# Cross attention on one Trainium2 core: the context turned by VectorE in 32x32 blocks, scores in four row groups, scores emitted ahead of the previous pair's weighted sum

## The chip, the cores and the metric

The kernel runs on one core of one Trainium2 chip. The metric is the device time of one execution in microseconds (us), and lower is better. TensorE (PE in the profile) multiplies matrices; PEld is its weight load. VectorE is DVE, ScalarE is ACT, GpSimd is POOL, and SP is the engine whose queue issues most of the transfers here. All of the data are float32 apart from the mask. A difference of less than about 0.3% can't be told from no change.

## The reference, cut to what matters

There are 32 sequences of 56 tokens with width 256, and each has its own context of 1500 rows by 256. Two layers run one after the other.

- Layer 0 first computes a decayed running sum over the context, projects its mean over time, adds it to every token of the sequence and normalises. Then comes a mixture of 16 experts of width 176, of which each token uses its six best.
- Layer 1 first attends from the tokens to the context, as below, and then uses the better of two experts of width 1024.

```python
scores = jnp.einsum('bsd,bmd->bsm', hidden_states, memory_tokens) * scale
scores = jnp.where(memory_mask[:, None, :], scores, neg_inf)
attn = jax.nn.softmax(scores, axis=-1)
readout = jnp.einsum('bsm,bmd->bsd', attn, memory_tokens)
```

The scores sum over the width (256), the readout sums over the context rows (1500). TensorE sums over the partitions of its operands, so the scores want the context with the width on the partitions, and the readout wants it with the rows on the partitions.

## The kernel before, in words

**Tiling.** Two sequences make a pair: rows 0 to 55 and 64 to 119 of a tile of 128 partitions. There are 16 pairs, in four groups of four. The residual of all tokens stays in SBUF (`xr`).

**Stage 1, the loads and the decayed sum (L123 to L281).** All 32 contexts are loaded once (`load_ctx`, L91), each with two transfers: 128 partitions with 11 rows of the context each, and 92 partitions with one row each. Four buffers take turns. For each context 12 matmuls in four column groups of the array add to `acc` (L205). The weights of layer 0's experts load in between (L200). A chain of small steps then gives the summary that L273 to L281 add to the tokens and normalise.

**Stage 2, layer 0's experts (L291, L384 to L449).** For each group of four pairs, 22 tiles of hidden units go through two matmul groups (L302), a SiLU on ScalarE (L307), two products on VectorE (L308, L310) and the projection back (L315). A float32 matmul shows as two instructions in the profile. The experts' weights per token are spread over the partitions by transfers on SP's queue, six tiles ahead (`cwb`). At a group's end the tokens are normalised, turned by TensorE and copied into `xnp` (L446), the queries of the attention, with the width on the partitions.

**Stage 3, the attention (L460 to L576).** For each pair:

- `transposed` (L469) turns each of the two contexts: 24 TensorE transposes of 128x128 each (L477) into PSUM, and six copies into `cT` by ScalarE (L486) and VectorE (L484).
- `mask_terms` (L489) loads the mask with two transfers, and POOL makes 0 or -1e30 of it (`mf`).
- `scores` (L505): three column blocks of at most 512, in two halves of the width, for the two sequences in the two column halves of the array (L514). VectorE adds the mask and takes the maximum (L520).
- `attend` (L527): the exponential on ScalarE (L530), 12 TensorE transposes of the weights (L541), VectorE's copies into `pT` (L545, L550), 24 matmuls with the context (L555), and the scaled sum into `xr` (L561). Then the next contexts but one are loaded into the freed buffers.

The Tile scheduler orders the instructions of each engine by its own simulation of the program. In the order that it gives to TensorE here, the transposes of the next pair's contexts stand among the steps of the current pair.

**Stage 4, layer 1's experts** (L580 to L620), with the same functions as stage 2, and the output.

**What sets the order around the change.** SP's queue issues the loads of contexts, masks and `cwb` in one order, and a transfer that has to wait for its buffer holds up those behind it. VectorE, ScalarE and POOL also take their instructions strictly in order.

## Time and profile before

| what | value |
|---|---|
| device time, median of three runs | 1325.13 us (1322.62 to 1326.71) |
| profiled execution: span | 1323.2 us |
| its own time | not given beside the span; the median of the runs lies 1.9 us above the span |
| PE busy | 1160.0 us, 88% of the span |
| DVE, ACT, POOL busy | 452.5, 250.5, 70.4 us |
| first context transpose of stage 3 (L477) | 658.78 us |
| last step of stage 3 (L561) | 1008.97 to 1009.45 us |
| contexts moved | 143.79 MB in all, of which 32 x 1.5 MB in stage 1 and again in stage 3 |

The span is the profiled execution from its first to its last instruction. A group's mean is the time of one instruction; on PE these overlap, so that busy time divided by count is less than the mean. PEclk is the share of its full clock that TensorE was granted.

### The profile page before, as it was taken

How to read it: one execution, taken by the hardware profiler on the slowest of the kernel's cores; microseconds unless marked ns; L12 is line 12 of the kernel's file. 1: busy time of each engine (PE TensorE's matmuls, PEld its weight loads, DVE VectorE, ACT ScalarE, POOL GpSimd, SP SyncE). 2: the span in 40 equal slices, each digit the busy share in tenths (PEclk: the TensorE clock that was granted, in tenths of full speed). 3: DMA queues.
4: the chain of work that ended last, by engine and by line, in shares of the span. 5: the costliest groups of instructions: out<-in, count | busy, mean ns of one | idle time of the engine just before them, and what ended most of it. 6: DMA issues, size and time to landing. Idle time of an engine off the chain costs nothing. (4 is left out here: it accounts for less than half of the span.)

```text
span 1323.2 us, 13044 instructions
## 1 busy us (share of the span) xinstructions
PE 1160.0 (88%) x5104; PEld 623.1 (47%) x5104; DVE 452.5 (34%) x1166; ACT 250.5 (19%) x412; POOL 70.4 (5%) x81
## 2 busy tenths in 40 slices
PE   5534455899999999999999998989898999999998
PEld 3111122455555555555445555656564545555554
DVE  2400008622532442332343443433434323232322
ACT  0000000211311321121143332323322111121111
POOL 1300002100000000000021011010100000000000
PEclk9576775799999999999999999999999999999999
DMA  9999990111111111111055345352520001000000
GB/s 304 332 340 338 346 321 35 49 65 56 42 50 51 47 50 49 49 53 53 18 204 198 145 154 185 113 189 108 192 94 15 15 0 28 0 28 1 14 0 14
DMA packets 38445, 143.79 MB, mean 109 GB/s; under 512 B 5031, under 2 KB 29168, under 8 KB 29424
## 3 DMA queue, kind: packets, MB, share of 16 engines
q1 hardware_dynamic: 35122, 134.03, 28.9%
q0 software_dynamic: 432, 6.29, 1.2%
q10 hardware_dynamic: 2830, 2.64, 0.8%
q8 instruction: 40, 0.66, 0.2%
q14 instruction: 21, 0.17, 0.0%
HBM read 140.98 MB, written 1.96 MB: 108 GB/s over the span
## 5 line engine op out<-in xcount | busy, mean ns | idle before, releaser
L302 PE MATMUL gp<-xnT,wg_sb 128*128 128x448 f32 x608 | 258.0, 543 | 0.0
L302 PE MATMUL up<-xnT,wu_sb 128*128 128x448 f32 x608 | 254.9, 540 | 0.0
L315 PE MATMUL y<-hh,wd_sb 128*128 128x448 f32 x608 | 254.3, 541 | 0.0
L308 DVE TENSOR_TENSOR sg<-sg,up 128x448 f32<-128x448 f32 x152 | 94.2, 620 | 422.0 <-PE up L302 417.3
L307 ACT ACTIVATE sg<-gp 128x448 f32<-128x448 f32 x152 | 82.3, 543 | 525.5 <-PE gp L302 517.8
L315 PEld LDWEIGHTS y<-hh,wd_sb 128*128 128x128 f32 x608 | 114.0, 190 | 112.4 <-issue 105.4
L302 PEld LDWEIGHTS up<-xnT,wu_sb 128*128 128x128 f32 x608 | 114.4, 191 | 106.7 <-issue 106.7
L205 PE MATMUL acc<-ctx,cz 128*32 128x256 f32 (+1 forms) x768 | 82.3, 562 | 93.7 <-DMA ctx<-in_cx 93.4
L302 PEld LDWEIGHTS gp<-xnT,wg_sb 128*128 128x128 f32 x608 | 113.7, 191 | 101.8 <-issue 101.8
L477 PE MATMUL tp<-ident,ctx 128*128 128x128 f32 (+1 forms) x768 | 113.5, 284 | 19.9 <-DMA ctx<-in_cx 10.8
L477 PEld LDWEIGHTS tp<-ident,ctx 128*128 128x128 f32 (+1 forms) x768 | 86.0, 145 | 63.1 <-ACT cT L486 18.4
L514 PE MATMUL sp<-cT,xnp 128*64 128x512 f32 (+1 forms) x384 | 103.0, 586 | 0.8 <-DVE mx L520 0.8
L205 PEld LDWEIGHTS acc<-ctx,cz 128*32 128x32 f32 (+1 forms) x768 | 32.5, 148 | 142.2 <-DMA ctx<-in_cx 119.3
L555 PE MATMUL op<-ctx,pT 128*64 128x256 f32 (+1 forms) x768 | 99.2, 387 | 0.0
L310 DVE TENSOR_TENSOR hh<-sg,cwb 128x448 f32<-128x448 f32 x152 | 94.8, 624 | 5.7 <-DMA cwb<-cw 1.0
L486 ACT COPY cT<-tp 128x512 f32<-128x512 f32 (+1 forms) x128 | 71.7, 569 | 96.0 <-PE tp L477 93.0
L555 PEld LDWEIGHTS op<-ctx,pT 128*64 128x64 f32 (+1 forms) x768 | 55.6, 138 | 31.1 <-issue 5.7
L484 DVE COPY cT<-tp 128x512 f32<-128x512 f32 x64 | 44.1, 689 | 73.1 <-PE tp L477 73.1
L514 PEld LDWEIGHTS sp<-cT,xnp 128*64 128x64 f32 x384 | 34.1, 136 | 47.1 <-issue 43.0
L110 ACT ACTIVATE rs<-mv,eps 128x4 f32<-128x4 f32 x20 | 5.9, 297 | 242.8 <-DVE mv L109 242.7
L530 ACT ACTIVATE sc<-sc,nb 128x1500 f32<-128x1500 f32 x16 | 24.8, 1547 | 118.6 <-DVE nb L529 118.6
L497 POOL TENSOR_SCALAR mf<-mu 128x1408 f32<-128x1408 uint8 x16 | 32.7, 2045 | 257.5 <-DVE mx L520 240.4
(116 smaller groups left out, 545.4 us busy)
## 6 DMA issues: line engine op xcount, KB each, us to landing
ctx<-in_cx SPq DMA_DIRECT2D x64, 1408.0 KB
cwb<-cw SPq DMA_DIRECT2D x40, 224.0 KB
ctx<-in_cx SPq DMA_DIRECT2D x64, 92.0 KB
cwb<-cw SPq DMA_DIRECT2D x16, 196.0 KB
mu<-in_mask SPq DMA_DIRECT2D x32, 93.8 KB
wg_sb<-in_wg SPq DMA_DIRECT2D x1, 2816.0 KB
wu_sb<-in_wu SPq DMA_DIRECT2D x1, 2816.0 KB
wd_sb<-in_wd SPq DMA_DIRECT2D x1, 2816.0 KB
```

The source lines that it names most:

```text
L205: PE.matmul(acc[32 * g : 32 * g + 32, :], lhsT=cz[0:r, j, B - 1 - b : 2 * B - 1 - b], rhs=c[0:r, j, :], start=(b == 0 and m == 0), stop=(b ...
L302: PE.matmul(o, lhsT=w[:, k, i * P : (i + 1) * P], rhs=xnT[:, k, :], start=(k == 0), stop=(k == KD - 1),)
L307: A.activation(sg, gp, AF.Silu)
L308: V.tensor_tensor(sg, sg, up, ALU.mult)
L310: V.tensor_tensor(hh, sg, weight(i), ALU.mult)
L315: PE.matmul(ys[k], lhsT=wd[:, i - 1, k * P : (k + 1) * P], rhs=hh, start=(i == 1), stop=(i == nf),)
L477: PE.transpose(tp[:, jj * P : jj * P + r], c[0:r, 4 * n + jj, k * P : (k + 1) * P], ident[0:r, 0:r],)
L484: V.tensor_copy(dst, tp[:, 0 : widths[n]])
L486: A.copy(dst, tp[:, 0 : widths[n]])
L497: G.tensor_scalar(mf[:, 0:TM].rearrange("q (j p) -> q j p", p=P), mu[:, 0:TM].rearrange("q (p j) -> q j p", j=TA), -1.0, BIG, ALU.add, ALU ...
L514: PE.matmul(sp[64 * h : 64 * h + 64, 0:w], lhsT=xnp[:, k, p * P + 64 * h : p * P + 64 * h + 64], rhs=cTs[h][:, k, cols], start=(k == 0), s ...
L555: PE.matmul(op[64 * h : 64 * h + 64, :], lhsT=pT[0:r, j, 64 * h : 64 * h + 64], rhs=ctxs[2 * p + h][0:r, j, :], start=(j == 0), stop=(j == ...
```

## The change

It is in stages 1 and 3, with a new transfer at the end of each group of stage 2.

- The context rows are laid out differently: row t = 12 p + j lies on partition p of 125, chunk j of 12. A load is now 112 partitions and 13 partitions of 12288 bytes each. Six fixed buffers replace four, and POOL sets their partitions 96 to 127 to zero once at the start.
- `transposed` becomes one VectorE instruction for each sequence and half of the width, four for a pair: each block of 32 partitions by 32 columns is turned in place. Afterwards partition 32 a + i holds column i of a 32-wide slice of the width, for the context rows of partition group a. So TensorE's transposes of the context, and ScalarE's and VectorE's copies of them, go.
- The scores now sum over 32 partitions at a time: eight slices e of the width, two sequences h, four row groups a, 64 matmuls of 384 (or 348) columns for a pair, into four PSUM tiles, one for each row group. The masked maximum is four VectorE instructions for a pair instead of three.
- The queries must stand on all four row groups in slices of 32. They go through DRAM: 16 writes at the ends of stage 2's groups (`xd`), and four reads for each pair (`queries`).
- The copies into `pT` move from VectorE to ScalarE, and `mf` has one buffer instead of two.
- TensorE's order in stage 3 is written out by hand: scores of pair p, weighted sum of pair p - 1, transposes of pair p's weights. The other engines' order is still the scheduler's.
- In stage 1 the summary is spread with two matmuls for each pair against a column of the identity, and the selection matrix that VectorE built before (`selb`) goes.

```diff
-    cpool = ctx.enter_context(tc.tile_pool(name="ctx", bufs=4))
+    cpool = ctx.enter_context(tc.tile_pool(name="ctx", bufs=1))
...
+    xd = dram.tile([D, NP, P], F32, name="xd")
+
+    cbuf = [cpool.tile([P, NCH, D], F32, tag=f"ctx{i}", name=f"ctx{i}") for i in range(NCTX)]
+    for c in cbuf:
+        G.memset(c[3 * Q : P], 0.0)
...
     def load_ctx(b):
-        c = cpool.tile([P, NCH, D], F32, tag="ctx", name=f"ctx{b}")
-        nc.sync.dma_start(
-            out=c[:, 0:TA, :], in_=cx[b, 0:TM, :].rearrange("(p j) d -> p j d", j=TA)
-        )
-        nc.sync.dma_start(out=c[0:TR, TA, :], in_=cx[b, TM:T, :])
+        c = cbuf[loads[0] % NCTX]
+        loads[0] += 1
+        cb = cx[b].rearrange("(p j) d -> p j d", j=NCH)
+        nc.sync.dma_start(out=c[0:TS], in_=cb[0:TS])
+        nc.sync.dma_start(out=c[TS:TP], in_=cb[TS:TP])
         return c
...
-                    A.copy(
-                        xnp[:, :, p * P : (p + 1) * P],
-                        tp[:, 0:D].rearrange("p (k c) -> p k c", c=P),
+                    xt = wk.tile([P, KD, P], F32, tag="xt", name="xt")
+                    A.copy(xt, tp[:, 0:D].rearrange("p (k c) -> p k c", c=P))
+                    nc.sync.dma_start(
+                        out=xd[:, GP * g + q, :].rearrange("(k p) c -> p k c", p=P), in_=xt
                     )
...
+        def transposed(b, n):
+            cT = ctp.tile([P, NCH, NE // 2, Q], F32, tag="cT", name="cT")
+            V.transpose(
+                out=cT.rearrange("p j e q -> p j (e q)"),
+                in_=ctxs[b][:, :, P * n : P * n + P],
+            )
             return cT
 
+        def queries(p):
+            xq = at2.tile([P, NE, P], F32, tag="xq", name="xq")
+            for a in range(4):
+                nc.sync.dma_start(
+                    out=xq[Q * a : Q * a + Q, :, :],
+                    in_=xd[:, p, :].rearrange("(e q) c -> q e c", q=Q),
+                )
+            return xq
...
+        def scores(p, cTs, xq, mf):
+            sps = [psc.tile([P, 512], F32, tag=f"sp{a}", name=f"sp{a}") for a in range(4)]
+            for e in range(NE):
+                for h in range(2):
+                    for a in range(4):
                         PE.matmul(
+                            sps[a][64 * h : 64 * h + 64, 0 : NCH * QT[a]],
+                            lhsT=xq[Q * a : Q * a + Q, e, 64 * h : 64 * h + 64],
+                            rhs=cTs[e // 4][h][Q * a : Q * a + Q, :, e % 4, 0 : QT[a]],
+                            start=(e == 0), stop=(e == NE - 1),
                         )
...
+        def turned(sc):
             pT = at.tile([P, NCH, P], F32, tag="pT", name="pT")
             for n in range(3):
                 tp = ppt.tile([P, 512], F32, tag="pt", name="tp")
                 for jj in range(4):
+                    PE.transpose(tp[0:TP, jj * P : (jj + 1) * P], sc[:, 4 * n + jj, :], ident)
+                A.copy(
+                    pT[0:TP, 4 * n : 4 * n + 4, :].rearrange("p j c -> p (j c)"), tp[0:TP, :]
+                )
+            return pT
...
+        with tc.manual_schedule(engines={mybir.EngineType.PE}):
+            before = None
+            for p in range(NP):
+                xq, mf = queries(p), mask_terms(p)
+                cTs = [[transposed(2 * p + h, n) for h in range(2)] for n in range(2)]
+                sc, mx = scores(p, cTs, xq, mf)
+                nb = softmax(sc, mx)
+                if before:
+                    attend(*before)
+                before = (p, turned(sc), nb)
+            attend(*before)
```

Here NCH = 12, TP = 125, Q = 32, NE = 8, TS = 112, NCTX = 6 and QT = [32, 32, 32, 29]. The tile pool of `cT` has four buffers, which is one pair's worth, that of the score tiles one for each row group.

## The prediction, made before the changed kernel ran

> **What bounds it now.** I read the busy times by stage first (columns: window, its length, busy time and count of each engine, granted TensorE clock, DMA share, GB/s).

> ```profile
> 0.00:196.00 196.00, 90.98 (x805) 40.95 (x806) 25.12 (x85) 3.96 (x7) 17.16 (x28) 0.71 0.93 329
> 238.00:658.00 420.00, 419.11 (x1215) 216.96 (x1214) 148.43 (x376) 81.71 (x135) 0.00 (x0) 0.99 0.16 49
> 658.00:1009.00 351.00, 323.03 (x2130) 195.57 (x2128) 141.86 (x378) 110.45 (x178) 39.74 (x36) 0.98 0.41 150
> 1009.00:1323.00 314.00, 306.86 (x912) 158.52 (x912) 102.01 (x225) 52.88 (x87) 0.00 (x0) 1.00 0.04 12
> ```

> Stage 1 waits for loads (DMA 0.93), stages 2 and 4 for TensorE. So does the attention (351 us, PE 92% busy, DVE 40%), and only there is something large removed. Next, that stage's groups of instructions by shape (busy us, mean ns | idle before):

> ```profile
> L477 PE MATMUL tp<-ident,ctx 128*128 128x128 f32 x704 | 109.1, 287 | 19.9 <-DMA ctx<-in_cx 10.8 <-DVE cT L484 6.5 <-ACT cT L486 1.8
> L555 PE MATMUL op<-ctx,pT 128*64 128x256 f32 x704 | 92.1, 388 | 0.0
> L514 PE MATMUL sp<-cT,xnp 128*64 128x512 f32 x256 | 74.4, 597 | 0.8 <-DVE mx L520 0.8
> L530 ACT ACTIVATE sc<-sc,nb 128x1500 f32<-128x1500 f32 x16 | 24.8, 1547 | 118.6 <-DVE nb L529 118.6
> L545 DVE COPY pT<-tp 128x512 f32<-128x512 f32 x32 | 21.3, 686 | 5.5 <-PE tp L541 5.3
> L545 DVE COPY pT<-tp 128x384 f32<-128x384 f32 x16 | 8.8, 552 | 3.1 <-PE tp L541 2.9
> ```

> Then one pair in order of time (start, duration):

> ```profile
> 782.23 1.07 PE L477 MATMUL tp<-ident,ctx 128*128 128x128 f32 x8 [0.80 <-DMA ctx<-in_cx]
> ...
> 792.63 5.18 PE L555 MATMUL op<-ctx,pT 128*64 128x256 f32 x45
> ...
> 797.66 0.34 SPq L93 DMA_DIRECT2D ctx<-in_cx  x1
> 797.86 5.20 PE L514 MATMUL sp<-cT,xnp 128*64 128x512 f32 x21
> ...
> 803.90 1.07 PE L477 MATMUL tp<-ident,ctx 128*128 128x128 f32 x8 [0.85 <-DMA ctx<-in_cx]
> 804.28 1.55 ACT L530 ACTIVATE sc<-sc,nb 128x1500 f32<-128x1500 f32 x1 [10.99 <-DVE nb L529]
> 805.97 0.77 PE L541 MATMUL tp<-ident,sc 128*128 128x128 f32 x5 [1.00 <-ACT sc L530]
> ```

> A pair takes 803.90 - 782.23 = 21.7 us (351 / 16 = 21.9 with the start and the end). TensorE's own prices: at 640 us four full-array matmuls of 448 columns start every 1.51 us, 0.84 ns a column, so a 128-column transpose costs 0.107 us; with two column groups side by side (L514, L555) a 512-column instruction costs 0.215, a 256-column one 0.108. Per pair: scores 24 x 0.215 = 5.2, context transposes 48 x 0.107 = 5.1, weight transposes 12 x 0.107 = 1.3, weighted sum 48 x 0.108 = 5.2, together 16.8; the rest is waits between steps. Last, the clock against idle TensorE:

> ```profile
> 105.00:107.00 2.00, 1.96 (x24) 0.81 (x24) 0.00 (x0) 0.00 (x0) 0.00 (x0) 1.00 0.97 382
> 997.20:1000.00 2.80, 0.00 (x0) 0.00 (x0) 1.03 (x5) 1.61 (x2) 0.95 (x1) 1.00 0.00 0
> 1001.20:1004.40 3.20, 2.88 (x14) 1.77 (x16) 1.61 (x4) 0.00 (x0) 0.00 (x0) 0.50 0.02 5
> ```

> After 2.9 us without matmuls the clock is 0.50 for 3.4 us. The first row has 24 matmuls of 256 columns in *four* column groups (L205) at full clock: 0.08 us each against 0.108 in two. Groups do run side by side.

> **The change, part by part.**

> *Context transposes go.* 768 x 0.107 = 82 us leave TensorE, with 128 ScalarE copies (72.8 us) and 64 VectorE copies (44.1 us). This would be the gain if TensorE stayed the bound; it does not, see below.

> *Scores in row groups.* 64 matmuls are 128 instructions of at most 384 columns, 384 x 0.84 = 0.32 us each. If all eight places (four row groups, two halves) run side by side, 16 steps x 0.32 = 5.1 us: the same as before. This trace has no row groups. Bounds: eight at once (like L205's four), 5.1; only the two halves at once, 64 x 0.32 = 20.5. I take 5.1, since L205's four groups start together at every step.

> *VectorE turns.* Four instructions of 1536 elements for a pair. No such operation is in the trace. Copies of 512 and 384 elements take 686 and 552 ns: 1.05 ns an element and 0.15 us fixed, so 1.76, or 1.7 back to back. Bounds: half of that per element (0.85) and two passes (3.4). I take 1.7.

> [...]

> *The new period.* In VectorE's order in the changed program, three of the next pair's turns stand before this pair's four maxima, and the fourth stands before the small operations that release the exponential. `cT` holds one pair, so a turn waits until the running scores have used its buffer. From the start of a pair's scores: half of the scores, 2.6 + 0.25 for the signal; three turns, 5.1; four maxima, 1.9 (512 elements follow each other every 0.61 us at 684.86; 0.13 less for 384); the fourth turn, 1.7; maximum, scale, signal, 0.45; exponential to first weight transpose, 805.97 - 804.28 = 1.7; 12 weight transposes with the wait for the first of ScalarE's copies, 1.75; then the next scores. Sum 15.5 us. TensorE works only 11.7 of it; the weighted sum hides behind maxima and turn, and then PE stands still for some 3.5 us, as long as the gap at 997. So I add 1.5 us for the granted clock (one window at 0.50 across transposes and first scores; 0 to 3), and 0.5 for loads: the next contexts are issued at 10.6 us and wanted at 18.4 and 20.1, where the first takes 803.90 - 797.66 = 6.2 us and both 3.07 MB some 10. Period 17.5 us (15.5 to 19.5).

> [...]

> *Start and end of the stage.* Queries now pass through DRAM: after the last experts (657.9) the last copy into the queries ends at 669.8 (L446), four writes and the reads each need some 2 us to land and 0.4 to issue, so scores start at 676.5, and TensorE idles meanwhile: 18.6 us. The turns of pair 0 hide in it. After the last pair's scores start, 15.5 + 0.9 + 5.2 + 0.5, with clock 23.5. Stage: 18.6 + 15 x 17.5 + 23.5 = 304.6 against 351: -46 us.

> *Query writes in stage 2.* 16 writes pass SP's queue among the `cwb` loads, and two `xt` buffers make ScalarE's third copy wait for the first write, with SiLUs queued behind. Cover: `cwb` is six tiles of 4.5 us ahead, the SiLU's tiles are double. I take +3 (0 to +8).

> *Stage 1.* Six zero fills on POOL (128x4096 takes 3.50 us at 1.78, so 2.6 each) delay the first context from 1.1 to 7.9 us and `cz` to 21; the expert weights (5.8 MB, 17 us at 329 GB/s) move ahead in SP's queue and fill the gap. Bytes are the same: 0 (-5 to +7). `selb`'s 2.2 us and the doubled summary matmuls lie beside loads or cancel: 0. The mask's single buffer is needed only every period: 0.

> **Sum.** 1323.2 - 46 + 3 = 1280 for the span; the median lies 1.9 above it: 1282 us.

> **Rivals.**

> - *Main case, chance 0.66:* as above, 1247 to 1318 with the periods 15.5 and 19.5 and stage 2's bounds.
> - *Four places at once instead of eight, 0.12:* scores take 10.2 us, the period is 20.6, the stage 355: 1332. For it: eight groups at once are nowhere in the trace.
> - *VectorE becomes the bound, 0.10 (the other side):* turns at 3.4 us make the period 23.6 and the stage 410, so 1387. It decides at 2.4 us a turn, where the period is 20.2 and the stage ends as before. Against it: the copies' slope.
> - *Row groups one after the other, 0.06:* period 30, the stage 506: 1483.
> - *Loads or stage 2 take the gain, 0.06:* 1305 to 1330. A load of 16 us makes the period 18.8, and 8 us more in stage 2 and 7 in stage 1.

> **How the numbers follow.** Faster: 0.66 and some of the last and second cases, 0.70; within 0.3% (4 us, what a measurement can tell) 0.03; slower 0.27. 1248 to 1342 holds the main case, the four-place one and the last: about 0.8 with their tails; the main case alone 1247 to 1318.

> **What would show it.** Scores of a pair: about 5 us from first to last start (10 or 20 in the rivals). A turn: 1.7 us. TensorE in the stage falls to about 70% busy, its waits ending at the exponential, with granted clock near 0.8; pairs follow each other every 17.5 us. VectorE's maxima wait behind turns. If the turns take over 2.4 us, or scores over 10, I am wrong.

## The result, and the profile after

The changed kernel takes 1397.95 us (1393.22 to 1410.86) against 1325.3 us before: a ratio of 1.057, 95% interval 1.052 to 1.062. It is slower by 5.7%, where 1282 us and a gain were forecast. The profiled execution's span is 1391.4 us against 1323.2.

First the same view that opened the prediction, busy times by stage, now of the kernel after. The columns are again window, length, busy time and count of PE, PEld, DVE, ACT and POOL, granted TensorE clock, DMA share and GB/s. The windows end at the last matmul of the decayed sum, the first expert matmul, the last matmul of layer 0's experts, the last of the weighted sum, and the end of the span.

```profile
0.00:258.50 258.50, 91.59 (x796) 42.61 (x796) 21.96 (x81) 3.96 (x7) 32.91 (x34) 0.67 0.99 243
258.50:305.50 47.00, 23.46 (x104) 11.76 (x104) 38.91 (x120) 1.79 (x6) 13.55 (x17) 0.54 0.61 150
305.50:731.00 425.50, 417.94 (x1198) 214.41 (x1197) 145.84 (x361) 82.33 (x136) 0.00 (x0) 0.99 0.17 52
731.00:1074.30 343.30, 235.88 (x3023) 156.62 (x3022) 171.80 (x345) 66.64 (x97) 38.23 (x20) 0.82 0.69 171
1074.30:1391.40 317.10, 310.06 (x912) 160.17 (x912) 102.05 (x225) 52.94 (x87) 0.00 (x0) 0.99 0.04 12
```

The same events in the trace of before lie at 193.5, 243, 659 and 1009 us. So:

| stage | before, us | after, us | difference | forecast difference |
|---|---|---|---|---|
| loads and decayed sum | 193.5 | 258.5 | +65.0 | 0 |
| the chain behind it | 49.5 | 47.0 | -2.5 | 0 |
| layer 0's experts | 416 | 425.5 | +9.5 | +3 |
| attention | 350 | 343.3 | -6.7 | -46 |
| layer 1's experts | 314 | 317.1 | +3 | 0 |

Look at the first row: DMA is busy 99% of the time, as one would wish of a stage that loads, and yet moves 243 GB/s. Before it moved 330 with a share of 0.93. The engines are full of slower transfers. The page of the kernel after shows it over the whole span (40 slices), and its chain of work puts a fifth of the span on the contexts' loads:

```profile
DMA  9999999922111112111107487797870000000000
GB/s 299 218 245 234 236 226 245 230 73 78 50 53 56 53 53 57 53 53 62 53 13 238 121 194 185 186 213 186 196 167 1 27 1 27 1 27 0 14 0 13
...
DMA ctx<-in_cx 20%; PE gp L297 17%; PE y L310 17%; PE up L297 16%; DVE cT L466 4%; PE sp L501 3%; DMA xr<-in_x 3%; PE tp L535 2%; DVE sc L511 2%; PE op L545 2%; DMA xd<-xt 1%; DVE xn L122 1%; PE lp L352 1%; ACT sc L523 1%; DVE st L113 1%
```

A packet is one contiguous piece of a transfer, here the row of one partition. In the trace a packet of 12288 bytes takes a median of 822 ns between 100 and 180 us (14.9 bytes a ns). Before, one of 11264 bytes took 427 there (26.4 bytes a ns).

What the change was forecast to do to the compute engines, it does. The groups by line of the kernel after (busy us, mean ns | idle before) give a VectorE turn of 1.76 us:

```profile
L466 DVE STREAM_TRANSPOSE cT<-ctx 128x1536 f32<-128x1536 f32 x64 | 110.9, 1761 | 134.9 <-PE sp L501 64.7
L501 PE MATMUL sp<-cT,xq 32*64 32x384 f32 (+1 forms) x2048 | 103.5, 544 | 18.6 <-DMA xq<-xd 18.6
```

And the timeline of the attention (start, duration; in brackets the idle time before, and what ended it) has two pairs that tell the rest:

```profile
815.03 5.53 PE L501 MATMUL sp<-cT,xq 32*64 32x384 f32 x128
...
818.05 1.78 DVE L466 STREAM_TRANSPOSE cT<-ctx 128x1536 f32<-128x1536 f32 x1 [5.78 <-PE sp L501]
820.12 3.44 DVE L466 STREAM_TRANSPOSE cT<-ctx 128x1536 f32<-128x1536 f32 x2 [0.29 <-DMA ctx<-in_cx]
...
825.92 0.33 SPq L103 DMA_DIRECT2D ctx<-in_cx  x1
...
832.15 5.50 PE L501 MATMUL sp<-cT,xq 32*64 32x384 f32 x128
...
835.14 1.78 DVE L466 STREAM_TRANSPOSE cT<-ctx 128x1536 f32<-128x1536 f32 x1 [5.75 <-PE sp L501]
841.51 3.44 DVE L466 STREAM_TRANSPOSE cT<-ctx 128x1536 f32<-128x1536 f32 x2 [4.59 <-DMA ctx<-in_cx]
...
853.67 6.68 PE L501 MATMUL sp<-cT,xq 32*64 32x384 f32 x128
```

The 128 score instructions of a pair take 5.5 us. Where the contexts arrive in time the next pair follows after 832.15 - 815.03 = 17.1 us. Where VectorE's second turn waits 4.59 us for the pair's second context (the pair's loads are issued from 825.92 on, and it is there at 841.5), the next follows after 853.67 - 832.15 = 21.5. Over all 16 pairs the period is 19.9 us, and VectorE's waits for contexts add up to 53.0 us.

### The profile page after: what moved, and what is told of

Same layout as the page of the kernel before. It is cut to its first block, busy times and chain, and to the rows that moved or that the text cites. A ratio compares the mean times of both kernels' runs of the same rounds, so it can differ in the third digit from the quotient of the medians.

```text
span 1391.4 us, 14910 instructions
## 1 busy us (share of the span) xinstructions
PE 1078.9 (78%) x6030; PEld 585.6 (42%) x6030; DVE 480.6 (35%) x1132; ACT 207.7 (15%) x332; POOL 84.7 (6%) x71
## 4 chain that ended last, share of the span: by engine, by line
PE 60%; DMA 26%; DVE 10%; issue 2%; ACT 1%; SPq 0%; ACTq 0%; DVEq 0%
DMA ctx<-in_cx 20%; PE gp L297 17%; PE y L310 17%; PE up L297 16%; DVE cT L466 4%; PE sp L501 3%; DMA xr<-in_x 3%; PE tp L535 2%; DVE sc L511 2%; PE op L545 2%; DMA xd<-xt 1%; DVE xn L122 1%; PE lp L352 1%; ACT sc L523 1%; DVE st L113 1%
## 5 line engine op out<-in xcount | busy, mean ns | idle before, releaser
L202 PE MATMUL acc<-ctx,cz 125*32 125x256 f32 x768 | 84.0, 605 | 148.7 <-DMA ctx<-in_cx 110.3
L466 DVE STREAM_TRANSPOSE cT<-ctx 128x1536 f32<-128x1536 f32 x64 | 110.9, 1761 | 134.9 <-PE sp L501 64.7
L501 PE MATMUL sp<-cT,xq 32*64 32x384 f32 (+1 forms) x2048 | 103.5, 544 | 18.6 <-DMA xq<-xd 18.6
L202 PEld LDWEIGHTS acc<-ctx,cz 125*32 125x32 f32 x768 | 35.2, 159 | 195.8 <-DMA ctx<-in_cx 132.2
L535 PE MATMUL tp<-ident,sc 128*125 128x128 f32 x192 | 45.1, 403 | 84.9 <-ACT sc L523 83.4
L545 PE MATMUL op<-ctx,pT 125*64 125x256 f32 x768 | 86.4, 381 | 0.0
L501 PEld LDWEIGHTS sp<-cT,xq 32*64 32x64 f32 x2048 | 63.9, 154 | 51.3 <-issue 20.4
L535 PEld LDWEIGHTS tp<-ident,sc 128*125 128x125 f32 x192 | 37.3, 284 | 95.5 <-ACT sc L523 90.4
L545 PEld LDWEIGHTS op<-ctx,pT 125*64 125x64 f32 x768 | 53.7, 137 | 34.5 <-issue 9.0
L490 POOL TENSOR_SCALAR mf<-mu 128x1500 f32<-128x1500 uint8 x16 | 35.5, 2217 | 281.9 <-DVE mx L511 274.6
```

What stands on the lines that cost most here:

```text
L202: PE.matmul(acc[32 * g : 32 * g + 32, :], lhsT=cz[0:TP, j, B - 1 - b : 2 * B - 1 - b], rhs=c[0:TP, j, :], start=(b == 0 and m == 0), stop= ...
L466: V.transpose(out=cT.rearrange("p j e q -> p j (e q)"), in_=ctxs[b][:, :, P * n : P * n + P],)
L490: G.tensor_scalar(mf, mu.rearrange("q (p j) -> q j p", j=NCH), -1.0, BIG, ALU.add, ALU.mult)
L501: PE.matmul(sps[a][64 * h : 64 * h + 64, 0 : NCH * QT[a]], lhsT=xq[Q * a : Q * a + Q, e, 64 * h : 64 * h + 64], rhs=cTs[e // 4][h][Q * a : ...
L535: PE.transpose(tp[0:TP, jj * P : (jj + 1) * P], sc[:, 4 * n + jj, :], ident)
L545: PE.matmul(op[64 * h : 64 * h + 64, 0:D], lhsT=pT[0:TP, j, 64 * h : 64 * h + 64], rhs=ctxs[2 * p + h][0:TP, j, :], start=(j == 0), stop=( ...
```

## The experiments

Theory A: the new shape of the loads is slow at the destination. A transfer of 112 partitions, if it is split evenly, gives each of 16 DMA engines 7 rows, and engines would then meet at the same part of SBUF. Theory B: the source is slow, since the rows of a transfer now lie 12288 bytes apart instead of 11264. Theory C: the second, 13-row transfer is to blame.

### Loads of 128 partitions in the kernel after

```diff
+        if b < B - 1:
+            cf = cx.rearrange("b t d -> (b t) d")[b * T : b * T + P * NCH, :]
+            nc.sync.dma_start(out=c, in_=cf.rearrange("(p j) d -> p j d", j=NCH))
+            return c
         nc.sync.dma_start(out=c[0:TS], in_=cb[0:TS])
         nc.sync.dma_start(out=c[TS:TP], in_=cb[TS:TP])
```

> The changed kernel, with each context but the last loaded in one transfer of 128 partitions (three rows of the next context come along and are not used: 2.4% more bytes), instead of 112 and 13 partitions. Theory A (destination: 112 partitions give each DMA engine 7 rows, and engines then meet at the same part of SBUF): 12288-byte packets fall from 825 ns to about 463 (11264 bytes take 424 before), the last matmul of the decayed sum comes at 197 to 205 us instead of 258, pairs follow at 17.1 us throughout, and the kernel takes 1280 to 1310 us. Theory B (source: a pitch of 12288 bytes between the rows of one transfer, instead of 11264, is slow to read): packets stay at about 825 ns and the time at 1395 to 1410. Theory C (the second, 13-row transfer holds up the engines): as A here.

Measured: 1274.4 us, ratio to before 0.964 (0.961 to 0.967). Packets take 462 ns, and the decayed sum ends at 176.0 us. By stage:

```profile
0.00:176.00 176.00, 74.10 (x796) 37.26 (x796) 22.00 (x81) 3.96 (x7) 32.95 (x34) 0.82 0.94 365
...
638.30:955.10 316.80, 234.99 (x3025) 155.73 (x3024) 171.21 (x345) 66.33 (x97) 38.38 (x20) 0.84 0.54 188
```

and in the middle of the loads:

```profile
100.00:140.00 40.00, 20.62 (x248) 8.03 (x240) 0.00 (x0) 0.00 (x0) 0.00 (x0) 0.76 1.01 426
```

426 GB/s at the same DMA share, with 2.4% more bytes. Rows of 12288 bytes are not slow to read, so B falls. With only the shape of the loads changed, a loss of 5.7% becomes a gain of 3.6%, more than theory A had forecast. The pairs follow each other at 17.0 to 19.0 us (the first 21.6, the last 20.3), 18.1 in the mean, not 17.1 throughout as I had written. Late contexts are the smaller part of that: VectorE waits 5.6 us for them in the whole stage. The longest period without such a wait, 19.0 us, has scores of 7.8 us instead of 5.4, at a granted clock of 0.50 in their first 4.3 us.

### The same cut put into the kernel before

```diff
-        nc.sync.dma_start(
-            out=c[:, 0:TA, :], in_=cx[b, 0:TM, :].rearrange("(p j) d -> p j d", j=TA)
-        )
+        cb = cx[b, 0:TM, :].rearrange("(p j) d -> p j d", j=TA)
+        nc.sync.dma_start(out=c[0:112, 0:TA, :], in_=cb[0:112])
+        nc.sync.dma_start(out=c[112:P, 0:TA, :], in_=cb[112:P])
```

> The kernel before, with its 128-partition transfer of a context cut into 112 and 16 partitions; all else as before. Theory A: 11264-byte packets rise from 424 to about 755 ns, the last matmul of the decayed sum moves from 193 to about 255 us, and the kernel takes 1385 us or more (up to 1480 if every pair of the attention also waits for its contexts). Theory B: nothing changes, 1323 to 1330. Theory C: 16 rows lie on 16 engines, one each, so little changes, under 1340.

The second kernel cuts at 64 instead of 112:

> The kernel before, with its 128-partition transfer cut into 64 and 64 partitions: each engine has 4 whole rows in each. Theory A in the form 'an uneven number of rows (7) per engine': nothing changes, 1323 to 1330. [...] Theory B: nothing changes.

The third cuts by rows within a partition and keeps 128 partitions:

```diff
+        nc.sync.dma_start(out=c[:, 0:6, :], in_=cb[:, 0:6])
+        nc.sync.dma_start(out=c[:, 6:TA, :], in_=cb[:, 6:TA])
```

> The kernel before, with its 128-partition transfer cut into two by rows of the context within a partition (6 and 5 of 11), so both keep 128 partitions. Theory A in the form 'engines meet at the same part of SBUF': packets of 6144 and 5120 bytes at about 231 and 193 ns (11264 take 424), and no change, 1320 to 1335. Rival (two large transfers for a context are slower than one, whatever their shape): packets near twice that and 1385 or more, as with 112 and 16, or 64 and 64 partitions.

Measured: 112 and 16 give 1462.9 us, a ratio of 1.107 (1.105 to 1.109); 64 and 64 give 1505.4 (one run); the cut within a partition gives 1326.6 (one run), no change. The same window of the loads, first before, then 112 and 16, then 64 and 64, then the cut within a partition:

```profile
100.00:180.00 80.00, 34.85 (x336) 13.05 (x336) 0.00 (x0) 0.00 (x0) 0.00 (x0) 0.68 0.91 337
```

```profile
100.00:180.00 80.00, 25.68 (x216) 10.55 (x216) 0.00 (x0) 0.00 (x0) 0.00 (x0) 0.56 0.94 217
```

```profile
100.00:180.00 80.00, 23.61 (x192) 9.47 (x192) 0.00 (x0) 0.00 (x0) 0.00 (x0) 0.56 0.93 188
```

```profile
100.00:180.00 80.00, 44.98 (x324) 15.34 (x324) 0.00 (x0) 0.00 (x0) 0.00 (x0) 0.72 0.95 336
```

Read the last column: 337, 217, 188, 336 GB/s. The cut of the change, with 16 rows in the second transfer for 13, costs the old kernel 10.7% by itself. An odd number of rows an engine isn't needed for it, since 64 and 64, where an even split gives 4, are worse. It is not the number of transfers or the size of packets either, since two transfers of smaller packets on 128 partitions lose nothing (336 GB/s for 337).

### Without the 13-row transfer

```diff
         nc.sync.dma_start(out=c[0:TS], in_=cb[0:TS])
-        nc.sync.dma_start(out=c[TS:TP], in_=cb[TS:TP])
```

> The changed kernel without the 13-partition transfer: 13 of each context's 125 partitions stay zero, so 10.4% of the bytes are left out. Theories A and B: packets stay near 800 ns, the last matmul of the decayed sum comes at about 234 us (10.4% less of 258.5 - 21), the kernel takes 1340 to 1365. Theory C: packets fall to about 460 ns, that matmul comes at about 180, and the kernel takes 1270 to 1290.

This kernel leaves out 13 partitions of each context. Measured (one run): 1335.5 us, packets of a median of 721 ns between 100 and 180 us, and the decayed sum ends at 222.6 us. The window from 100 to 160 us:

```profile
100.00:160.00 60.00, 32.53 (x288) 11.56 (x288) 0.00 (x0) 0.00 (x0) 0.00 (x0) 0.51 1.01 274
```

Theory C alone is out, since 274 is far from 426. But the end came 11 us earlier than A gives for the bytes alone, and in this window the kernel after moves 236. So the 13-row transfer may do some harm of its own. How much isn't shown: from 180 to 240 us this kernel moves 252, and the 112-row loads moved 246 when they ran alone (below).

### Only transfers: destination or source?

This kernel leaves out all arithmetic. It makes 16 loads in each of five shapes, one shape after another (name, first partition, partitions, context rows in each):

```
("full", 0, 128, 11), ("sevens", 0, 112, 12), ("low", 0, 64, 22), ("middle", 32, 64, 22), ("sixes", 0, 96, 14)
out=c[lo : lo + n, 0:r, :], in_=cx[b, 0 : n * r, :].rearrange("(p j) d -> p j d", j=r)
```

> Only transfers, everything else is left out (the output is zeros): 16 contexts each in five shapes, one after the other. full: partitions 0-127, 11 rows of the context each (packets of 11264 bytes); sevens: 0-111, 12 rows (12288); low: 0-63, 22 rows (22528); middle: the same source rows and packets as low, but to partitions 32-95; sixes: 0-95, 14 rows (14336). Theory 'destination' (engines meet at the same part of SBUF): full 415 to 430 GB/s, sevens 240 to 290, low 215 or less, and middle near 400, since only the first partition differs from low; 22528-byte packets 1.6 us in low and about 0.85 in middle. [...] Theory 'source or row count' (fewer, longer rows, or their pitch in DRAM): low and middle the same. sixes has no partner and shows how far 6 rows an engine are from 7.

The windows of this kernel (one run), one inside each shape (only POOL is listed, then clock, DMA share, GB/s):

```profile
5.00:40.00 35.00, 0.00 (x0) 1.00 1.01 426
70.00:130.00 60.00, 0.00 (x0) 1.00 1.01 246
150.00:250.00 100.00, 0.00 (x0) 1.00 1.00 206
262.00:305.00 43.00, 0.00 (x0) 1.00 1.00 430
320.00:400.00 80.00, 0.00 (x0) 1.00 1.01 225
```

The third and fourth rows move the same source rows in the same packets of 22528 bytes. Only the first partition differs, 0 or 32, and the rate differs by 430 / 206 = 2.1 (packets 1756 and 839 ns). The slow transfers are slowed at the destination: that is shown. Partitions 0 to 63 are slow, 32 to 95 and 0 to 127 are not, 0 to 111 and 0 to 95 are nearly as slow as 0 to 63.

No earlier run had shown that 32 to 95 would be fast: the 400 GB/s expected of it was an estimate, and 430 was measured. Why these two ranges differ isn't shown.

An estimate for 112 and 96 partitions: if their first 64 moved at the measured 206 GB/s and the others beside them in no more time, 206 x 112 / 64 = 360 and 206 x 96 / 64 = 309 GB/s would be left. The 246 and 225 are the measurement's own. So slow partitions 0 to 63 alone don't explain them, and that engines meet at the same part of SBUF stays an assumption of theory A, not seen. Why 112 and 96 are that slow stays open; that they are slow is shown.

### The remainder of the kernel before

The kernel before moved 330 to 348 GB/s (348 from 100 to 160 us), and the 128-partition shape 426. Its second transfer has 92 rows, so it was widened:

```diff
-        nc.sync.dma_start(out=c[0:TR, TA, :], in_=cx[b, TM:T, :])
+        if b < B - 1:
+            cf = cx.rearrange("b t d -> (b t) d")[b * T + TM : b * T + TM + P, :]
+            nc.sync.dma_start(out=c[:, TA, :], in_=cf)
+        else:
+            nc.sync.dma_start(out=c[0:TR, TA, :], in_=cx[b, TM:T, :])
```

> The kernel before, with its 92-row transfer widened to 128 rows (36 rows of the next context come along, unused). Theory: 92 rows lie unevenly on the 16 engines, which is why the kernel before loads at 330 GB/s where the 128-row shape reaches 425; the last matmul of the decayed sum comes 10 to 20 us earlier (174 to 184 instead of 193.5), the attention is not changed (its loads are in time), and the kernel takes 1303 to 1316 us. Rival: the clock of TensorE or the small packets set the rate: no change, 1320 to 1328.

Measured: 1296.0 us, ratio 0.979 (0.975 to 0.983), the decayed sum ends at 167.5 us instead of 193.5, and the attention takes 347.9 us.

```profile
100.00:160.00 60.00, 27.22 (x292) 10.33 (x288) 0.00 (x0) 0.00 (x0) 0.00 (x0) 0.69 1.02 420
```

More bytes in less time: 26 us for an edit that touches no arithmetic, more than the 10 to 20 forecast. So part of the gain of the first experiment belongs to the loads, not to the attention.

Why the wider transfer helps isn't shown: the trace doesn't name the engines, and that 92 rows lie unevenly on them stays an estimate. Three figures bear on it. The packets got no faster (medians 46 ns for 1024 bytes and 425 to 427 for 11264 in both kernels), so it isn't the slow destination of the section before. The DMA share between 100 and 160 us went from 0.93 to 1.02. And between 100 and 150 us, of the time in which any 1024-byte packet is in flight, more than four are in flight in 1% with 92 rows and in 18% with 128.

### Is it the order of TensorE?

```diff
-                if before:
-                    attend(*before)
-                before = (p, turned(sc), nb)
-            attend(*before)
+                attend(p, turned(sc), nb)
```

> The kernel with contexts loaded in 128 rows, but scores not ahead: each pair's scores follow the weighted sum of the pair before. Theory (the period is set by VectorE's turns and the softmax, and TensorE stands idle in it): scores 5.6 + 0.3, maxima 1.9, small steps 0.45, exponential 1.7, weight transposes 1.8, weighted sum 5.4 make 17.1; three turns still stand ahead of the maxima and add up to 2, so a period of 17 to 19.5 and 1265 to 1305 us. Rival (the emission ahead hides the weighted sum, 5.4 us a pair): 1274 + 16 x 5.4 = 1360.

Measured: 1352.0 us, ratio 1.021 (1.018 to 1.024), 78 us more than with scores ahead. My theory missed. The rival, 1360, is 8 us too high and right in kind. One period of its timeline:

```profile
809.49 5.41 PE L505 MATMUL sp<-cT,xq 32*64 32x384 f32 x128
...
812.36 5.10 DVE L470 STREAM_TRANSPOSE cT<-ctx 128x1536 f32<-128x1536 f32 x3 [1.57 <-PE sp L505]
...
817.38 0.52 DVE L515 CUSTOM_DVE_ANT_1 sc<-sp,mf 128x384 f32<-128x384 f32 x1
...
819.23 1.77 DVE L470 STREAM_TRANSPOSE cT<-ctx 128x1536 f32<-128x1536 f32 x1
...
821.27 1.54 ACT L527 ACTIVATE sc<-sc,nb 128x1500 f32<-128x1500 f32 x1 [16.42 <-DVE nb L526]
...
822.96 3.16 PE L539 MATMUL tp<-ident,sc 128*125 128x128 f32 x12 [8.06 <-ACT sc L527]
826.05 6.36 PE L549 MATMUL op<-ctx,pT 125*64 125x256 f32 x48
```

Half of the scores 2.9, three turns 5.0, maxima 1.85, fourth turn and small steps 2.0, exponential 1.7, transposes 3.1 (at half clock, after 8.06 us without matmuls), weighted sum 6.3: 22.85, and the next scores start at 832.34. My sum for this kernel forgot the fourth turn and the clock. The chain is the one that the prediction wrote down, with the weighted sum at its end instead of beside it. The emission ahead is worth 5 us a pair.

This kernel also shows something of the clock. In the period before the one shown, a window without matmuls, one with nothing but transposes, and what follows:

```profile
797.40:800.70 3.30, 0.00 (x0) 0.00 (x0) 1.97 (x6) 1.33 (x1) 2.20 (x1) 0.50 0.82 128
800.80:804.10 3.30, 3.04 (x12) 2.69 (x12) 0.32 (x2) 1.38 (x4) 0.00 (x0) 0.50 0.16 59
804.20:806.00 1.80, 1.80 (x19) 1.22 (x20) 0.00 (x0) 0.58 (x1) 0.00 (x0) 1.00 0.00 0
```

In this period the clock is back from 0.50 to 1.00 after the 12 transposes alone, and the weighted sum behind them takes 5.4 us; in the period shown above it takes 6.4, so the clock comes back later there.

### Are the eight places needed side by side?

```diff
-            for e in range(NE):
-                for h in range(2):
-                    for a in range(4):
+            for a in range(4):
+                for e in range(NE):
+                    for h in range(2):
```

> The kernel with 128-row loads, but with the four row groups' scores emitted one group after the other (the loop over the groups outermost), so that neighbouring instructions only differ in the column half. Theory (eight places run side by side only when neighbours use different places): the 128 score instructions take about 20.5 us a pair instead of 5.5, all turns then wait for the last group, and the period is 20.5 + 0.3 + 5.1 + 1.9 + 1.7 + 0.45 + 1.7 + 1.75 = 33.4 instead of 17.6: 1500 to 1550 us. Rival (the order does not matter, the pieces overlap anyway): scores stay near 5.5 and the time at 1274.

Measured (one run): 1606.7 us; scores take 28.1 us a pair (27.7 to 33.2), and the pairs follow each other at 37.4 to 43.3 us:

```profile
942.35 28.12 PE L505 MATMUL sp<-cT,xq 32*64 32x384 f32 x128
```

A window inside these scores, with TensorE busy throughout:

```profile
950.00:955.00 5.00, 5.00 (x24) 2.07 (x24) 0.00 (x0) 0.00 (x0) 0.00 (x0) 0.50 0.09 24
```

So here neighbouring instructions had to use different row groups for eight to run side by side: 5.5 against 28 us for the same 128 instructions. The 20.5 of the prediction's bound was short because the clock fell: weight loads follow each other in steps of 0.32 us early in a pair's scores (905.27, 905.59) and of 0.64 later (910.05, 910.69). It fell although TensorE didn't stand idle (5.00 of 5.00 us busy at 0.50).

### The query writes

The start of the attention was 26 us in the kernel after, where 18.6 were forecast. Its timeline:

```profile
731.08 0.75 POOL L453 DMA_DIRECT2D wg_sb<-in_wg  x1 [431.79 <-PE tp L325]
...
736.86 15.56 SPq L442 DMA_DIRECT2D xd<-xt  x4
...
751.15 0.65 ACT L441 COPY xt<-tp 128x256 f32<-128x256 f32 x2 [13.99 <-DMA xd<-xt]
...
753.99 3.44 DVE L466 STREAM_TRANSPOSE cT<-ctx 128x1536 f32<-128x1536 f32 x2 [17.20 <-DMA xd<-xt]
```

Layer 1's weights, 6.3 MB in three transfers, go out 5 us ahead of the query writes. It takes 15.6 us to issue the four writes, since ScalarE's third copy waits 13.99 us until the first write has landed. A first try moved the weights' emission to the second pair, with the 128-row loads:

```diff
-    for sb, w in ((wg1_sb, wg1), (wu1_sb, wu1), (wd1_sb, wd1)):
-        nc.gpsimd.dma_start(out=sb, in_=w)
+                if p == 1:
+                    for sb, w in ((wg1_sb, wg1), (wu1_sb, wu1), (wd1_sb, wd1)):
+                        nc.gpsimd.dma_start(out=sb, in_=w)
```

> The kernel with contexts loaded in 128 rows, and the weights of layer 1 (6.3 MB, issued by POOL at the end of layer 0's experts) issued after the second pair's mask instead. Theory: the first query write took 14.15 us to land because it stood behind these weights on the DMA engines; without them it lands in about 2 us, the first scores start 12 us earlier after the last expert, and the kernel takes about 1262 us (1257 to 1268). Rival: the write is slow by itself (512-byte pieces): the time stays at 1274. Second rival: the weights now collide with the first contexts of the attention and cost there what was gained: 1270 to 1276.

It measured 1278.7 us, ratio 0.967 (0.964 to 0.971), but it decided nothing: nothing held the weights back, and the scheduler still issued them at 641.7, 653.4 and 654.0 us, around the query writes. On top of that the six zero fills were taken out:

> The one before, and without the six zero fills on POOL (with 128-row loads the rows that they filled are loaded). Theory: the fills let the scheduler put the first normalisation, which waits for x until 54 us, ahead of the copies that start the decayed sum, so six buffers were full and the DMA engines idle for some 8 us; without the fills the sum starts near 17 us and ends at 160 to 168 us instead of 176, and the kernel takes 1247 to 1255 (8 to 14 us less than with late weights alone). Rival: the bytes alone set the end of the loads: no change against late weights alone.

It measured 1273.4 us, ratio 0.962 (0.959 to 0.964). The first matmul of the decayed sum moved from 56.5 to 15.8 us, as expected, but its end only from 176.2 to 172.0, against 160 to 168 forecast: the bytes were nearly the limit already (DMA share 0.97 over these 172 us). Then POOL's order was written out by hand as well, which keeps the weights behind the second pair's mask:

```diff
-        with tc.manual_schedule(engines={mybir.EngineType.PE}):
+        with tc.manual_schedule(engines={mybir.EngineType.PE, mybir.EngineType.Pool}):
```

> The kernel with 128-row loads and no fills, with the weights of layer 1 now kept behind the second pair's mask in POOL's own order, so that they can't start before the first pair's maxima (the earlier try left them at 641 us, ahead of the query writes). Theory: the query writes land in about 2 us each, the first scores start about 19 us after the last expert instead of 31, and the kernel takes 1258 to 1264 us (10 to 15 less than 1273). Rival: the weights now hold up the queries, masks and contexts of the second to fourth pair by their own 15 us: no gain, 1268 to 1276.

Measured: 1264.3 us, ratio 0.956 (0.953 to 0.960), the fastest kernel here. Its timeline:

```profile
643.79 3.79 SPq L444 DMA_DIRECT2D xd<-xt  x4
649.13 12.97 SPq L476 DMA_DIRECT2D xq<-xd  x10
...
652.12 9.04 PE L501 MATMUL sp<-cT,xq 32*64 32x384 f32 x128 [7.19 <-DMA xq<-xd]
...
696.17 1.78 DVE L466 STREAM_TRANSPOSE cT<-ctx 128x1536 f32<-128x1536 f32 x1 [8.22 <-DMA ctx<-in_cx]
```

The four writes are issued in 3.8 us instead of 15.5, and the first scores start 15.9 us after the last expert (636.2). About 6 us of that are given back where the weights, which land until 689.6, delay the contexts of the fourth pair, issued from 684.9 on: the third period is 23.4 us.

### Six buffers for turned contexts

```diff
-        name="ctxT", bufs=4
+        name="ctxT", bufs=6
```

> The kernel with 128-row loads, late weights and no fills, and six buffers for turned contexts instead of four (room for them from one buffer less for the scores, the normed rows and the small tiles). Theory: two of the next pair's turns no longer wait for half of the scores and all four stand before the maxima, so the chain from scores to scores falls from 15.5 to about 12.5 us; with TensorE's own 12.7 a pair and clock losses the period is 13 to 15 instead of 17.6, and the kernel takes 1195 to 1220 us. Rival (contexts arrive too late, 10.5 us after their issue, or the lower clock takes it): the period stays above 16.5 and the time within 15 us of the one without the six buffers.

Measured: 1271.9 us, ratio 0.960 (0.957 to 0.964), the same as without them (1273.4). The rival holds, and the timeline says how:

```profile
774.50 6.84 PE L501 MATMUL sp<-cT,xq 32*64 32x384 f32 x128
...
789.47 5.41 PE L501 MATMUL sp<-cT,xq 32*64 32x384 f32 x128
...
794.36 1.78 DVE L466 STREAM_TRANSPOSE cT<-ctx 128x1536 f32<-128x1536 f32 x1 [5.54 <-DMA ctx<-in_cx]
800.06 5.10 DVE L466 STREAM_TRANSPOSE cT<-ctx 128x1536 f32<-128x1536 f32 x3 [3.92 <-DMA ctx<-in_cx]
...
812.27 6.73 PE L501 MATMUL sp<-cT,xq 32*64 32x384 f32 x128
```

Where contexts are there, the period is 15.0 us here and 12.9 to 14.3 elsewhere, as the theory had it. Then two turns wait 5.5 and 3.9 us for contexts issued at 786.7, and the next period is 22.8. Six context buffers hold three pairs, and a load can only be issued when a pair's weighted sum is done. The mean stays at 18.5 us.

## Why the prediction was wrong

**The step that failed** is "*Stage 1.* [...] Bytes are the same: 0 (-5 to +7)", with its echo "0.5 for loads" in the period. I priced the loads by their bytes at the rate of before, and left out what their new shape does to the rate. Measured: stage 1 +65 us and its chain -2.5, and periods that wait for contexts. The first experiment shows that both go with the shape. The rival "*Loads or stage 2 take the gain*" had the right mechanism and too small a price (7 us in stage 1; it ended at 1330). The other rivals didn't come true; the stage of 410 in the one on VectorE doesn't follow from its own period of 23.6, which gives 18.6 + 15 x 23.6 + 23.5 + 6.1 = 402 us.

**The whole difference, step by step.** Forecast span 1280, measured 1391.4:

- Loads and chain of stage 1: +62.5 instead of 0.
- Layer 0's experts +9.5 instead of +3. With 128-row loads the same code takes 415.3 us, 0.7 less than before. So the query writes cost nothing there, and the loss goes with the slow loads; by which wait isn't shown.
- Attention 343.3 instead of 304.6. Its start is 25.8 instead of 18.6 (+7.2). The period is 19.87 instead of 17.5 (15 x 2.37 = +35.5). The end is 19.7 instead of 23.5 (-3.8): the forecast let four turns stand in the chain after the last scores, and after the last pair there are none.
- Layer 1's experts +3 instead of 0. They take 314 us in some of these kernels and 317 in others, without a cause that I could name.

**What was right.**

- "*Context transposes go*": PE busy fell from 1160.0 to 1078.9 us, and the stage had not stayed TensorE's (236 busy of 343).
- "*Scores in row groups*": 5.5 us a pair for 5.1; the serial order shows the rest.
- "*VectorE turns*": 1.76 us for 1.7. That is what the copies' 1.05 ns an element and 0.15 us fixed gave.
- "*The new period*": where contexts are in time, mostly 17.1 to 17.5 us in the kernel after and 17.0 to 19.0 in the repaired one (mean 17.6), for 17.5. Term by term, from 815.03 to 832.15: half of the scores 3.0, three turns 5.4, maxima 1.9, fourth turn and small steps 2.0, exponential 1.7, transposes 3.1, where the sum had 2.85, 5.1, 1.9, 2.15, 1.7 and 1.75. What it allowed for the clock, 1.5, shows mostly in the transposes, and the granted clock of the stage is 0.82, close to the 0.8 foretold.
- "*Start and end of the stage*" failed in one term: the first write, "some 2 us" to land (an estimate), took some 14 (and the four 15.6 to issue), behind weights that I had not looked for in POOL's queue. The last experiment on it shows that as the cause: with the weights later, the first write is issued at 643.79 and the copy that waits for it starts at 646.31, 2.5 us later.

**With the loads repaired** the forecast would have stood: 1274.4 us against 1282. But two errors cancel there. The loads gain 17.5 us over before, which nobody forecast, and the attention saves 33 instead of 46: 304.6 + 7.7 (start 26.3) + 9.6 (period 18.14) - 5.1 (end 18.4) = 316.8.

**What the change itself is worth.** Against the kernel before with its own loads repaired (1296.0), the best version (1264.3) is 2.4% faster. That comes from the attention, first that of the kernel before with its loads repaired, then that of the best version:

```profile
632.80:980.70 347.90, 321.20 (x2128) 194.07 (x2128) 141.99 (x377) 109.67 (x177) 39.77 (x36) 0.99 0.41 154
636.20:949.00 312.80, 236.16 (x3024) 156.71 (x3023) 172.71 (x345) 66.48 (x97) 38.34 (x20) 0.85 0.55 191
```

With the loads alone repaired on both sides (1274.4 against 1296.0), the change is worth 1.7% (1.5% by the two ratios to before).

## What to carry to other kernels

Price a load by its shape, not only by its bytes: which partitions it covers (430 GB/s to partitions 32 to 95 here, 206 to 0 to 63), and how many rows each of its transfers has (420 GB/s with 128 rows in the second transfer, 348 with 92). A DMA share of 0.99 beside a low 243 GB/s was the sign here, and the duration of a packet in the trace, set against its bytes, says it at once (822 ns for 12288 bytes in the kernel after, 462 with 128 partitions). Where a layout doesn't fill 128 partitions, loading unused rows to fill them can be cheaper than the exact shape: here 2.4% more bytes took 176 us instead of 258.5. And when a step begins to use a queue, look at what every other queue has just handed to the DMA engines: here 6.3 MB of weights stood ahead of a write that took some 14 us.
